# First pair's results held in DRAM by rows and copied out later, one more residual tile, Layer 1 sums by units of one group

## The chip, the core and the metric

The kernel runs on one core of one Trainium2 chip. The metric is device time of one execution in microseconds. TensorE is called PE, VectorE DVE, ScalarE ACT, GpSimd POOL and SyncE SP. SP and ACT each issue DMA transfers into a queue of their own (in the profile, q1 is SP's and q10 is ACT's); both queues run on the same 16 DMA engines.

## The reference

Two layers of the same form: `x = x + scan(groupnorm(x))`, float32 throughout. The scan passes a 48x48 convolution with five taps, along rows and then along columns, each step adding the convolution of the line before to the next line.

```python
def f(carry, inp):                       # one step of a scan
    nxt = inp + _conv1d(carry, w, b)     # 48 channels, 5 taps, padding 2
    return (nxt, nxt)

# x: (32, 48, 64, 128) = batch, channel, row h, column w
xs = jnp.moveaxis(x, 2, 0)
D = scan(down_w, xs)                     # 63 steps over h, downwards
U = scan(down_w, D reversed)             # 63 steps, upwards
R = scan(right_w, columns of U)          # 127 steps over w, to the right
L = scan(left_w, R reversed)             # 127 steps, to the left

def _gn(v, G=16, eps=1e-5): ...          # mean and variance over 3 channels x 64 x 128 of an image
x = x + conv(_gn(x), L0 weights)
x = x + conv(_gn(x), L1 weights)
```

A layer's second half can begin only when the whole image has been summed, since the norm needs its mean and variance. The steps of one scan depend on each other, so the work is a chain of 2 x 4 scans, and it is filled by working on several images at once.

## The kernel before, in words

**Tiling.** The 32 images are four groups of 8. For the row scans a group is worked on alone: 126 steps, each step on a line of 128 columns. For the column scans two groups, a *pair*, go together: 254 steps (127 to the right, 127 to the left). Eight channels-by-position blocks of 48 are packed into 3 x 128 partitions (the table PIECES gives the ten pieces, of 48, 32 or 16 partitions), and a step is 9 fp32 matmuls into 3 PSUM tiles (L641) and 3 DVE instructions that add bias and input (L650). PE and DVE alternate; nothing else is on this chain.

**Phases.** The table PHASES has twelve: eight of rows (group 0 to 3, layer 0 and 1) and four of columns. In what follows they are numbered from 0: phase 2 and phase 6 are the column scans of layer 0, phase 10 that of layer 1 for the *first pair* (images 0 to 15), phase 11 that of layer 1 for the *second pair*. Phase 11 is the last. PE instructions are named by phase: `step_10r` and `step_10l` are the right and the left scan of phase 10 (layer 1, pair 0), `step_11r` and `step_11l` those of phase 11 (layer 1, pair 1); `step_00r` and `step_01r` open phases 2 and 6; `step_00d` and `step_01d` are the downward scans of phases 0 and 1.

**Storage.** One SBUF tile, `arena`, holds three *slots* (each a half image by rows, or one *quarter* of the columns of a pair) and four staging tiles of 2048 floats per partition. A column phase needs four quarters (j = 0 to 3, 32 columns each) and has three slots: quarter 0 and quarter 3 share a slot, so quarter 0 is written to DRAM (`spill`) once the right scan has passed it and is brought back for the left scan. A quarter is six *units* of 128 partitions x 2048 floats (1.05 MB); unit (o, half) is third o of the partitions for one group of the pair. Row results go to the DRAM tensors `upa` and `upb` (layer 0 and 1), the input in the kernel's order to `xin`, layer 0's result to `mid`. Since a column quarter of `upa` can be read only when every row has been written, the start of a column phase that directly follows the rows of its second group (phases 2 and 6) loads that group in parts (L790 on): first the rows 16 to 63, then 8 to 15, then 0 to 7.

**Results of layer 1** (phases 10 and 11). When the left scan is through with a quarter (order 3, 2, 1, 0), each of its six units gets its residual loaded from `mid` into a staging tile (`load_residual`, on ACT's queue), POOL adds scan result and residual and at the same time puts the elements into the order of the output (`add_permuted`, L614, eight instructions of 128x256), and the sum goes from a second staging tile to the output (`store_result`). Two staging tiles hold residuals, two hold sums. In this version a unit of layer 1 is half of the rows of *both* groups of the pair, so a store is cut into 4 x 3 or 4 x 4 transfers, half of them on SP's queue and half on ACT's. The output has 32 floats (128 bytes) in one piece for one image, channel, row and quarter: 49,152 pieces a quarter, 196,608 a pair. For the last quarter of phase 11 the residuals go into a slot that has come free (`last_loads`), DVE adds, and ACT, POOL and DVE reorder (`last_results`, L872 and L880).

**Order.** Nothing is scheduled at run time. `at(t, fn, ...)` (L720) puts a call on a list with a time t, counted in scan steps from the program's start; before each step is recorded, all calls that are due are recorded (`catch_up`, L1047). This fixes the order on each engine and each queue. A queue issues in that order: an instruction that must wait for data or for a buffer holds up all behind it in its queue. `starts[k]` is the step at which phase k begins; in a column phase `left` is the step at which the left scan begins and `end` the one after its last.

**The first group.** Group 0's input is read, reordered, written to `xin` in DRAM and brought back by rows in the first phase; `move_rows` brings rows in, `scale_rows` applies the norm on ACT (L525), and `take_in` reads group 1's input.

## Time and profile before

| | before |
|---|---|
| median of 10 runs | 4554.6 us (4549.24 to 4560.19) |
| the profiled execution's own time | 4552.77 us |
| its span (first to last instruction) | 4551.0 us |
| mean granted TensorE clock | 0.963 |
| PE busy | 4161.9 us (91%) |
| DVE, ACT, POOL busy | 2183.6, 1183.2, 907.9 us (48%, 26%, 20%) |
| DMA | 661.55 MB, 2124132 packets, of them 2010816 under 512 B |

How to read it: the profile is of one execution. "Busy" is time in which an engine runs an instruction; a row of waits names the engine, the line, what ended the wait, and the time in total. In a timeline, the figure in brackets is the idle time just before the row. In a table of windows, each engine has its busy time and, in brackets, its instructions in that stretch; then come PEclk, the clock that TensorE was granted (1.00 is full speed), the share of time that the 16 DMA engines were busy (over 1 where packets of two queues overlap), and what they moved in GB/s. The DMA view of a window gives packets and bytes, and the transfers issued with their median time to landing. The releaser that a wait names is inferred: "DVE L650" before a matmul can stand for a transfer that came late.

### The profile page before, as it was taken

The numbers are of one execution on the slowest core, as the hardware profiler recorded it, in microseconds if no ns is written. First come the engines' busy times: TensorE is split into PE (matmuls) and PEld (weight loads), VectorE is DVE, ScalarE is ACT, GpSimd is POOL, SyncE is SP. The second block draws the span as 40 slices with busy tenths as digits, with TensorE's granted clock in tenths as the row PEclk, the third lists the DMA queues.
The fourth block names the chain that finished last, engine by engine and source line by source line (L and its number), as shares of the span: only waits on it lengthen the run. The fifth ranks groups of instructions, "written<-read, shape, count | busy, mean of one in ns | idle before, by whom it ended". The sixth has DMA issues, their size and how long they took to land.

```text
span 4551.0 us, 90798 instructions
## 1 busy us (share of the span) xinstructions
PE 4161.9 (91%) x36632; PEld 4130.6 (91%) x36632; DVE 2183.6 (48%) x6594; ACT 1183.2 (26%) x2334; POOL 907.9 (20%) x943
## 2 busy tenths in 40 slices
PE   4889998999999999979999999999999997869980
PEld 2889998999999999979999999999999997869980
DVE  5454443446655444434456654444444443334441
ACT  1553302426776445000025944330000000000000
POOL 4441001314412020000024300000000155500554
PEclk9999998999999999989999999999999998989995
DMA  8989789847979999389038989384790199970799
GB/s 178 175 164 156 114 147 198 198 101 244 215 162 162 159 156 158 67 152 201 2 92 241 205 143 152 49 142 82 119 215 2 22 198 179 206 175 1 155 167 160
DMA packets 2124132, 661.55 MB, mean 145 GB/s; under 512 B 2010816, under 2 KB 2063808, under 8 KB 2092224
## 3 DMA queue, kind: packets, MB, share of 16 engines
q1 hardware_dynamic: 1901312, 573.92, 66.1%
q10 hardware_dynamic: 222400, 81.83, 9.5%
q8 instruction: 288, 4.72, 0.5%
q14 instruction: 132, 1.08, 0.1%
HBM read 378.70 MB, written 277.11 MB: 144 GB/s over the span
## 4 chain that ended last, share of the span: by engine, by line
PE 79%; DMA 12%; SPq 3%; ACT 2%; POOL 1%; issue 1%; ACTq 1%; DVE 1%; POOLq 0%; DVEq 0%
PE step_00r L641 6%; PE step_01r L641 6%; PE step_10r L641 6%; PE step_00l L641 6%; PE step_01l L641 6%; PE step_10l L641 5%; DMA arena<-mid 4%; PE step_11r L641 3%; DMA out<-arena 3%; SPq L182 3%; PE step_11l L641 3%; PE step_11d L641 3%; PE step_02u L641 3%; PE step_10u L641 3%; PE step_11u L641 3%; PE step_12d L641 3%
## 5 line engine op out<-in xcount | busy, mean ns | idle before, releaser
L525 ACT ACTIVATE arena<-arena,offset,scale 128x256 f32<-128x256 f32 (+2 forms) x840 | 594.6, 802 | 445.3 <-DMA arena<-xin 181.3
L614 POOL TENSOR_TENSOR arena<-arena 128x256 f32<-128x256 f32 x336 | 349.5, 1080 | 976.2 <-DVE arena L650 714.5
L482 POOL COPY arena<-arena 112x256 f32<-112x256 f32 x458 | 270.8, 650 | 758.5 <-DMA arena<-in_x 427.0
L880 ACT COPY arena<-arena 128x256 f32<-128x256 f32 x18 | 10.5, 643 | 1474.8 <-DMA out<-arena 1471.8
L594 POOL TENSOR_TENSOR arena<-arena 128x2048 f32<-128x2048 f32 x48 | 217.7, 4562 | 839.3 <-PE step_01l L641 543.6
L641 PE MATMUL step_11r<-arena,wright 128*128 128x128 f32 x2286 | 265.3, 280 | 89.0 <-DVE arena L650 42.1
L641 PEld LDWEIGHTS step_11r<-arena,wright 128*128 128x128 f32 x2286 | 263.5, 196 | 90.8 <-DVE arena L650 59.0
L416 ACT ACTIVATE junk<-arena 128x256 f32<-128x256 f32 x192 | 129.5, 675 | 703.6 <-DMA arena<-xin 563.6
L641 PE MATMUL step_01r<-arena,wright 128*128 128x128 f32 x2286 | 258.7, 277 | 29.5 <-DMA arena<-upa 29.5
L641 PEld LDWEIGHTS step_01r<-arena,wright 128*128 128x128 f32 x2286 | 258.4, 194 | 29.8 <-issue 29.6
L641 PE MATMUL step_00r<-arena,wright 128*128 128x128 f32 x2286 | 258.9, 277 | 28.7 <-DMA arena<-upa 28.7
L641 PEld LDWEIGHTS step_00r<-arena,wright 128*128 128x128 f32 x2286 | 258.5, 194 | 29.1 <-issue 28.9
L641 PE MATMUL step_00l<-arena,wleft 128*128 128x128 f32 x2286 | 256.3, 275 | 0.0
L641 PE MATMUL step_10r<-arena,wright 128*128 128x128 f32 x2286 | 256.1, 275 | 0.0
L641 PEld LDWEIGHTS step_10r<-arena,wright 128*128 128x128 f32 x2286 | 255.7, 192 | 0.3
L641 PEld LDWEIGHTS step_00l<-arena,wleft 128*128 128x128 f32 x2286 | 255.7, 192 | 0.0
L641 PE MATMUL step_01l<-arena,wleft 128*128 128x128 f32 x2286 | 255.4, 275 | 0.0
L641 PE MATMUL step_10l<-arena,wleft 128*128 128x128 f32 x2286 | 255.4, 275 | 0.0
L641 PE MATMUL step_11l<-arena,wleft 128*128 128x128 f32 x2286 | 255.4, 275 | 0.0
L641 PEld LDWEIGHTS step_01l<-arena,wleft 128*128 128x128 f32 x2286 | 255.3, 192 | 0.0
L641 PEld LDWEIGHTS step_10l<-arena,wleft 128*128 128x128 f32 x2286 | 255.3, 192 | 0.0
L641 PEld LDWEIGHTS step_11l<-arena,wleft 128*128 128x128 f32 x2286 | 255.3, 192 | 0.0
(173 smaller groups left out, 6990.3 us busy)
## 6 DMA issues: line engine op xcount, KB each, us to landing
xin<-arena SPq DMA_DIRECT2D x96, 384.0 KB, 5.4
arena<-xin SPq DMA_DIRECT2D x96, 384.0 KB, 8.6
mid<-arena SPq DMA_DIRECT2D x96, 384.0 KB, 7.9
arena<-mid SPq DMA_DIRECT2D x192, 192.0 KB, 4.3
upb<-arena SPq DMA_DIRECT2D x192, 192.0 KB, 3.9
arena<-mid ACTq DMA_DIRECT2D x192, 192.0 KB, 4.6
arena<-upb SPq DMA_DIRECT2D x96, 384.0 KB, 10.9
arena<-xin SPq DMA_DIRECT2D x186, 192.0 KB, 4.3
```

The lines of the kernel that those rows point to most:

```text
L182: (queue or nc.sync).dma_start(dst, src)
L416: nc.scalar.activation(junk[:, 0:n], view[:, b], AF.Identity, accum_out=self.sum[:, i, j : j + 1])
L482: copy(dst[:, r, q], src[:, r0 + r, q])
L525: nc.scalar.activation(args[0], args[0], AF.Identity, bias=args[2], scale=args[1])
L594: nc.gpsimd.tensor_tensor(unit, unit, nat, ALU.add)
L614: engines[(2 * a + s) % len(engines)].tensor_tensor(dst[:, a, s], res[:, a, s], inp[:, a, s], ALU.add)
L641: nc.tensor.matmul(part(whole(ps[o]), -s), weights[:, i, FULL * (o - NG * s - i + 1) : FULL * (o - NG * s - i + 2)], part(src(i), s), star ...
L880: copy(dst[:, a, s], src[:, a, s])
```

## The change

Six edits, all in the plan and in the helpers of layer 1's results; no matmul and no DVE instruction of a scan changes.

1. **Units.** In layer 1 a unit is now (third, group), as in layer 0: `load_residual` moves 8 KB rows in 3 or 4 transfers, and `store_result` writes a unit with 3 or 4 transfers, all on SP's queue. The bytes and the 128-byte pieces in the output stay.
2. **Held results.** For the first pair, quarters 2, 1 and 0 are not stored to the output. `hold_result` writes each summed unit as it lies, 128 partitions x 8 KB, to a DRAM tensor (ACT's queue). Later `let_result` copies from DRAM to the output: 48 transfers of 384 KB on SP's queue, listed from 63 steps after phase 11's start on, 1.9 steps apart.
3. **Third residual tile.** The weights of the row scans, which have done their work by then, lie in one tile `downs`; 2048 of its 2304 floats per partition serve as third tile for residuals in both column phases of layer 1.
4. **A gate on ACT.** Ten steps into the left scan of phases 10 and 11, ACT copies one element that the left scan writes at its seventh step; ACT's residual loads stand behind it.
5. **Phases 2 and 6.** The second group's rows 32 to 63 are loaded 31 steps before the phase, rows 16 to 31 13 steps before it; they went together 13 steps before.
6. **First group.** Rows 56 to 63 are brought in together with 48 to 55, ahead of group 1's first input, and scaled in two halves, due 26 and 32 steps into phase 0 (one call due at 34 before).

Three places show the order. In the rows, `out<-held` is a copy from DRAM to DRAM, `mid` the residuals, `upb` and `upa` row results, `spill` quarter 0.

SP's queue at the end of phase 11's loads, before the left scan. Before, the stores of the second pair follow the loads directly:

```order
L182 DMA arena<-upb_97 32x2048
L182 DMA arena<-upb_97 48x2048 x2
L182 DMA arena<-upb_98 32x2048
L182 DMA arena<-upb_98 48x2048 x2
L182 DMA out<-arena 48x16x32 x2
L182 DMA out<-arena 32x16x32
```

Now:

```order
L192 DMA arena<-upb_96 32x2048
L192 DMA arena<-upb_96 48x2048 x2
L192 DMA arena<-upb_97 32x2048
L192 DMA arena<-upb_97 48x2048 x2
L192 DMA out<-held_108 384x8x32 x8
L192 DMA out<-held_109 384x8x32 x8
L192 DMA out<-held_110 384x8x32 x8
L192 DMA out<-held_111 384x8x32 x8
L192 DMA out<-held_112 384x8x32 x8
L192 DMA out<-held_113 384x8x32 x8
L192 DMA out<-arena 384x8x32 x2
```

The 48 copies stand between the last load of phase 11 and the first store of its results, which is behind them in the queue.

ACT's queue in phase 10's left scan. Before, the rows of two units: residual loads and a store's half in turn:

```order
L182 DMA arena<-mid_87 16x1024
L182 DMA arena<-mid_88 16x1024
L182 DMA out<-arena 48x16x32 x2
L182 DMA out<-arena 32x16x32
L182 DMA out<-arena 48x16x32 x2
L182 DMA out<-arena 32x16x32
L182 DMA arena<-mid_87 16x1024
L182 DMA arena<-mid_88 16x1024
L182 DMA arena<-mid_87 48x1024
L182 DMA arena<-mid_88 48x1024
```

Now, in quarter 2:

```order
L192 DMA held_108<-arena 128x2048
L192 DMA arena<-mid_86 32x2048
L192 DMA arena<-mid_86 48x2048 x2
L192 DMA held_109<-arena 128x2048
L192 DMA downs<-mid_87 32x2048
L192 DMA downs<-mid_87 48x2048 x2
```

A unit's store has become one transfer to DRAM, with a residual load of larger rows between two of them; every third residual goes to `downs`.

ACT's queue ahead of phase 2. Before:

```order
L525 ACTIVATE arena<-arena,offset_2822,scale_2821 128x256 x96
L182 DMA arena<-upa_92 48x1536 x2
L182 DMA arena<-upa_92 32x1536
L182 DMA arena<-upa_92 16x1536
L182 DMA arena<-upa_92 48x1536 x2
L182 DMA arena<-upa_92 16x1536
```

Now:

```order
L535 ACTIVATE arena<-arena,offset_2851,scale_2850 128x256 x96
L192 DMA arena<-upa_91 48x1024 x2
L192 DMA arena<-upa_91 32x1024
L192 DMA arena<-upa_91 16x1024
L192 DMA arena<-upa_91 48x1024 x2
L192 DMA arena<-upa_91 16x1024
```

Two thirds of each early load now stand 18 steps earlier; ten transfers of 512 floats follow them at the old place.

The diff:

```diff
--- before.py
+++ after.py
@@ -136,7 +136,9 @@
     arena = const([FULL, 3 * SLOT + 4 * UNIT], "arena")
     slot = [arena[:, i * SLOT : (i + 1) * SLOT] for i in range(3)]
     stage = arena[:, 3 * SLOT :].rearrange("p (i n) -> p i n", i=4)
-    wt = {k: const([FULL, NG, NG * FULL], f"w{k}") for k in ("down0", "down1", "right", "left")}
+    wt = {k: const([FULL, NG, NG * FULL], f"w{k}") for k in ("right", "left")}
+    downs = const([FULL, 2, NG, NG * FULL], "downs")
+    wt |= {f"down{i}": downs[:, i] for i in range(2)}
     bd = const([FULL, NG, 2, 3], "bd")
     mask_sb = const([P, P], "mask_sb")
     maskp = const([P, NG, FULL], "maskp")
@@ -161,6 +163,14 @@
         dram.tile([2 * NG, FULL, UNIT], F32, tag=f"spill{i}", name=f"spill{i}")
         for i in range(4)
     ]
+    HELD = (2, 1, 0)
+    held = {
+        (j, half): dram.tile([NG, FULL, UNIT], F32, tag=f"held{j}{half}", name=f"held{j}{half}")
+        for j in HELD
+        for half in range(2)
+    }
 
     def by_row(t, e, h0, h1):
 
@@ -565,28 +575,12 @@
         else:
             dma(there, here)
 
-    HH = NH // 2
     def load_residual(k, j, i, nat):
         _, layer, pair = PHASES[k]
-        if layer == 0:
-            o, half = UNITS[i]
-            t = source[0][2 * pair + half]
-            for e, c0, c1, p0 in pieces(o):
-                dma(nat[p0 : p0 + c1 - c0], by_col(t, e, j)[c0:c1])
-            return
-        o, r = divmod(i, 2)
-        view = nat.rearrange("p (s n) -> p s n", s=2)
-        part = slice(r * HH * LINE, (r + 1) * HH * LINE)
+        o, half = UNITS[i]
+        t = source[layer][2 * pair + half]
         for e, c0, c1, p0 in pieces(o):
-            for s in range(2):
-                dma(
-                    view[p0 : p0 + c1 - c0, s],
-                    by_col(source[1][2 * pair + s], e, j)[c0:c1, part],
-                    nc.scalar,
-                )
+            dma(nat[p0 : p0 + c1 - c0], by_col(t, e, j)[c0:c1], nc.scalar if layer else None)
 
     def add_residual(k, j, i, nat):
         o, half = UNITS[i]
@@ -602,29 +596,41 @@
                 quarter(k, j)[p0 : p0 + c1 - c0, half, o],
             )
 
-    def add_permuted(k, j, i, nat, perm, engines):
-        o, r = divmod(i, 2)
-        res = quarter(k, j)[:, :, o].rearrange(
-            "p s (a e k b) -> p a s b k e", a=NH, e=E8, b=GB
-        )[:, r * HH : (r + 1) * HH]
-        inp = nat.rearrange("p (s a e k b) -> p a s b k e", s=2, a=HH, e=E8, b=GB)
-        dst = perm.rearrange("p (a s b k e) -> p a s b k e", a=HH, s=2, b=GB, e=E8)
-        for a in range(HH):
-            for s in range(2):
-                engines[(2 * a + s) % len(engines)].tensor_tensor(
-                    dst[:, a, s], res[:, a, s], inp[:, a, s], ALU.add
-                )
+    def by_image(t):
+        return t.rearrange("p (a e k b) -> p a b k e", a=NH, e=E8, b=GB)
+    def by_w(t):
+        return t.rearrange("p (a b k e) -> p a b k e", a=NH, b=GB, e=E8)
+    def add_permuted(k, j, i, nat, perm):
+        o, half = UNITS[i]
+        res = by_image(quarter(k, j)[:, half, o])
+        for a in range(NH):
+            nc.gpsimd.tensor_tensor(by_w(perm)[:, a], res[:, a], by_image(nat)[:, a], ALU.add)
+    def in_output(j, g, e):
+        t = out[g * GB : (g + 1) * GB].rearrange("b c (a e) w -> e (c a) b w", e=E8)
+        return t[e, :, :, j * WQ : (j + 1) * WQ]
 
     def store_result(k, j, i, perm):
         pair = PHASES[k][2]
-        o, r = divmod(i, 2)
-        both = out[2 * pair * GB : 2 * (pair + 1) * GB]
-        dst = both.rearrange("b c (a e) w -> e a c b w", e=E8)[..., j * WQ : (j + 1) * WQ]
-        src = perm.rearrange("p (a b n) -> p a b n", a=HH, b=2 * GB)
-        for a in range(HH):
-            for e, c0, c1, p0 in pieces(o):
-                to = nc.sync if a < HH // 2 else nc.scalar
-                dma(dst[e, r * HH + a, c0:c1], src[p0 : p0 + c1 - c0, a], to)
+        o, half = UNITS[i]
+        for e, c0, c1, p0 in pieces(o):
+            dst = in_output(j, 2 * pair + half, e)[c0 * NH : c1 * NH]
+            src = perm[p0 : p0 + c1 - c0].rearrange("p (a b n) -> p a b n", a=NH, b=GB)
+            dma(dst.rearrange("(c a) b n -> c a b n", a=NH), src)
+    def hold_result(j, i, perm):
+        o, half = UNITS[i]
+        dma(held[j, half][o], perm, nc.scalar)
+    def let_result(j, half, e):
+        src = held[j, half].rearrange("o p (a b n) -> (o p a) b n", a=NH, b=GB)
+        dma(in_output(j, half, e), src[e * C * NH : (e + 1) * C * NH])
 
 
     def step(key, weights, b_at, src, inp, dst, whole, part):
@@ -794,7 +800,8 @@
         for i in range(n):
             if follows(k) and UNITS[i][1] == 1:
                 other = nc.scalar
-                at(t0 - 13 + i, load_unit, k, 0, i, 2, NH, 0, E8, other)
+                at(t0 - 31 + i, load_unit, k, 0, i, 4, NH, 0, E8, other)
+                at(t0 - 13 + i, load_unit, k, 0, i, 2, 4, 0, E8, other)
                 at(t0 - 6 + i / n, load_unit, k, 0, i, 1, 2, 0, E8, other)
                 at(t0 - 1.5, load_unit, k, 0, i, 0, 1, E8 // 4, E8, other)
                 at(t0, load_unit, k, 0, i, 0, 1, 0, E8 // 4, other)
@@ -822,6 +829,8 @@
             stats = ResultStatsV(f"r{2 * pair}"), ResultStatsA(f"r{2 * pair + 1}")
         tiles = [stage[:, i] for i in range(4)]
         nats, perms = (tiles, None) if layer == 0 else (tiles[0:2], tiles[2:4])
+        if layer:
+            nats.append(downs.rearrange("p i g n -> p (i g n)")[:, 0:UNIT])
         ahead = len(nats)
 
         for u, (t, j, i) in enumerate(units):
@@ -842,13 +851,23 @@
                     at(t + 1, stats[1].take, j, o, unit)
             elif not (final and j == 0):
                 perm = perms[u % 2]
-                at(t, add_permuted, k, j, i, nat, perm, [nc.gpsimd])
-                at(t + 5, store_result, k, j, i, perm)
+                at(t, add_permuted, k, j, i, nat, perm)
+                if final or j not in HELD:
+                    at(t + 5, store_result, k, j, i, perm)
+                else:
+                    at(t + 5, hold_result, j, i, perm)
         if layer == 0:
             t = units[-1][0] + 14
             g = 2 * pair
             spread(t, scaling(f"r{g}", 1, g, stats[0], r_masks), 1)
             spread(t + 20, scaling(f"r{g + 1}", 1, g + 1, stats[1], r_masks), 1)
+        if layer:
+            at(left + 10, nc.scalar.copy, junk[:, 0:1], quarter(k, 3)[:, 0, 0, RUN - 1 : RUN])
+        if layer and not final:
+            todo = [(j, half, e) for j in HELD for half in range(2) for e in range(E8)]
+            for n, what in enumerate(todo):
+                at(end + 63 + 1.9 * n, let_result, *what)
         if final:
             at(left + 97, last_loads, k)
             at(end + 4, last_results, k)
@@ -865,19 +884,14 @@
     def last_results(k):
 
         for i, nat in enumerate(last_tiles(k)):
-            o, r = divmod(i, 2)
-            part = slice(r * HH * LINE, (r + 1) * HH * LINE)
-            unit = quarter(k, 0)[:, :, o, part]
-            nat = nat.rearrange("p (s n) -> p s n", s=2)
+            o, half = UNITS[i]
+            unit = quarter(k, 0)[:, half, o]
             nc.vector.tensor_tensor(unit, unit, nat, ALU.add)
-            src = unit.rearrange("p s (a e k b) -> p a s b k e", a=HH, e=E8, b=GB)
             perm = stage[:, i % 4]
-            dst = perm.rearrange("p (a s b k e) -> p a s b k e", a=HH, s=2, b=GB, e=E8)
-            for a in range(HH):
-                for s in range(2):
-                    eng = (nc.scalar, nc.gpsimd, nc.vector)[(2 * a + s) % 8 % 3]
-                    copy = eng.copy if eng is nc.scalar else eng.tensor_copy
-                    copy(dst[:, a, s], src[:, a, s])
+            for a in range(NH):
+                eng = (nc.scalar, nc.gpsimd, nc.vector)[a % 3]
+                copy = eng.copy if eng is nc.scalar else eng.tensor_copy
+                copy(by_w(perm)[:, a], by_image(unit)[:, a])
             store_result(k, 0, i, perm)
 
 
@@ -1032,14 +1046,14 @@
         scale_rows(0, 24, 32)
         move_rows(0, 32, 48, False)
         scale_rows(0, 32, 40)
-        move_rows(0, 48, 56, False)
+        move_rows(0, 48, 64, False)
         take_in(1, 0, nats1[0])
 
     in_order(first_group)
     at(starts[0] + 10, scale_rows, 0, 40, 48)
-    at(starts[0] + 20, move_rows, 0, 56, 64, False)
     at(starts[0] + 22, take_in, 1, 16, nats1[1])
-    at(starts[0] + 34, scale_rows, 0, 48, 64)
+    at(starts[0] + 26, scale_rows, 0, 48, 56)
+    at(starts[0] + 32, scale_rows, 0, 56, 64)
 
     agenda.sort(key=lambda a: a[:2])
     done = 0
```

## The prediction

> **What bounds the kernel now.** I read the table of windows first, one window for each scan of the last two phases and one for the tail (columns: window, length, busy time of PE, PEld, DVE, ACT, POOL, then granted clock, DMA share, GB/s).
>
> ```profile
> 3560.00:3815.00 255.00, 255.00 (x2286) 255.00 (x2285) 121.85 (x381) 0.00 (x0) 113.64 (x109) 1.00 0.72 139
> 3815.00:4170.00 355.00, 266.01 (x2296) 264.21 (x2295) 123.24 (x383) 0.00 (x0) 86.33 (x84) 0.87 0.76 150
> 4170.00:4425.00 255.00, 254.84 (x2283) 254.65 (x2281) 121.78 (x381) 0.00 (x0) 116.59 (x112) 1.00 0.69 136
> 4425.00:4551.00 126.00, 0.00 (x0) 0.00 (x0) 23.35 (x19) 10.46 (x18) 49.44 (x50) 0.51 1.02 162
> ```
>
> A column scan that nothing disturbs is PE's: 255 us for 127 steps, 2.01 a step. The right scan of phase 11 takes 355, 100 too many, and after the last step 126 us pass with no matmul while the DMA share is 1.02. These are the two places with much to win. Then the PE timeline over the 355 us, with the idle time and its releaser in brackets:
>
> ```profile
> 3789.78 25.62 PE L641 MATMUL step_10l<-arena,wleft 128*128 128x128 f32 x228
> 3829.47 1.22 PE L641 MATMUL step_11r<-arena,wright 128*128 128x128 f32 x4 [13.62 <-DMA out<-arena]
> 3848.34 66.57 PE L641 MATMUL step_11r<-arena,wright 128*128 128x112 f32 x570 [17.65 <-DMA arena<-mid]
> 3918.90 1.65 PE L641 MATMUL step_11r<-arena,wright 128*128 128x128 f32 x6 [3.98 <-DVE arena L650]
> 3936.20 65.16 PE L641 MATMUL step_11r<-arena,wright 128*128 128x112 f32 x568 [15.65 <-DMA arena<-mid]
> 4009.98 0.79 PE L641 MATMUL step_11r<-arena,wright 128*128 128x128 f32 x2 [8.62 <-DVE arena L650]
> 4031.06 1.65 PE L641 MATMUL step_11r<-arena,wright 128*128 128x128 f32 x6 [20.29 <-DVE arena L650]
> 4041.88 127.69 PE L641 MATMUL step_11r<-arena,wright 128*128 128x112 f32 x1126 [9.18 <-DVE arena L650]
> ```
>
> Three waits, before steps 1, 32 and 64 (32 steps are 576 matmuls): each is for the next quarter of phase 11, which is loaded into a slot that phase 10's results must leave first. They are 31.3, 19.6 and 38.1 us, 89.0 together. By the page's groups the scan's matmuls are also 10 us longer in sum than those of the left scan, which has no waits and the full clock; so the waits cost 99.
>
> ```profile
> L641 PE MATMUL step_11r<-arena,wright 128*128 128x128 f32 x2286 | 265.3, 280 | 89.0 <-DVE arena L650 42.1 <-DMA arena<-mid 33.3 <-DMA out<-arena 13.6
> L641 PE MATMUL step_11l<-arena,wleft 128*128 128x128 f32 x2286 | 255.4, 275 | 0.0
> ```
>
> The DMA view of the stretch says what the loads wait behind:
>
> ```profile
> DMA  3998889999897999999999999999999999999999
> DMA packets 216494, 88.35 MB, mean 198 GB/s; under 512 B 205738, under 2 KB 205738, under 8 KB 211882
> ```
>
> From 3620 to 4066 the DMA engines are busy throughout, and 205,738 of the packets are small: phase 10's output, which by the code is 196,608 pieces of 128 bytes. Between that and the next stretch the engines are idle (4080 to 4215):
>
> ```profile
> DMA  0000000000000000000000000000000000000000
> DMA packets 12, 0.18 MB, mean 1 GB/s; under 512 B 0, under 2 KB 0, under 8 KB 0
> ```
>
> **Edit 2, 3 and 4 in the right scan of phase 11.** Prices first, each from a window with one kind of transfer: the last stores (4500 to 4540), residual loads alone (4421 to 4449), loads of 128-byte pieces from DRAM (1520 to 1540), and spills of 128 partitions x 8 KB to DRAM (3362 to 3378).
>
> ```profile
> DMA packets 52002, 6.51 MB, mean 163 GB/s; under 512 B 52000, under 2 KB 52000, under 8 KB 52000
> ```
>
> ```profile
> DMA packets 1840, 5.28 MB, mean 189 GB/s; under 512 B 551, under 2 KB 551, under 8 KB 1840
> ```
>
> ```profile
> DMA packets 24988, 3.17 MB, mean 159 GB/s; under 512 B 24987, under 2 KB 24987, under 8 KB 24987
> ```
>
> ```profile
> DMA packets 649, 4.74 MB, mean 296 GB/s; under 512 B 72, under 2 KB 72, under 8 KB 72
> ```
>
> Three quarters are 147,456 pieces; at 52,002 in 40 us they take 113 us of the DMA engines. They leave the stretch. In come 18 held units of 1.05 MB, 18.9 MB; the form is that of a spill, 64 us at 296 GB/s. That window includes some loads and an idle start, so 64 is the upper bound; I take 55. The gate keeps two units' residuals of phase 11 (2.1 MB, 11 us at 189 GB/s) out of the stretch; ACT issued them there (its timeline, 12 transfers):
>
> ```profile
> 3995.39 14.33 ACTq L182 DMA_DIRECT2D arena<-mid  x12
> ```
>
> Net: 113 - 55 + 11 = 69 us less DMA work ahead of the third wait. It ended at 4041.9; 69 earlier is 3973. Without waits step 64 is due at 3815 + 64 x 2.01 = 3944, so by work alone 29 us of waiting stay, and the gain is 69.
>
> It should be more, since the DMA engines can also do this work faster. In the last left scan, where the same mechanism runs, POOL shows how a unit is paced:
>
> ```profile
> 4383.28 8.31 POOL L614 TENSOR_TENSOR arena<-arena 128x256 f32<-128x256 f32 x8 [5.31 <-DMA arena<-mid]
> 4396.86 8.30 POOL L614 TENSOR_TENSOR arena<-arena 128x256 f32<-128x256 f32 x8 [5.26 <-DMA arena<-mid]
> 4410.01 8.31 POOL L614 TENSOR_TENSOR arena<-arena 128x256 f32<-128x256 f32 x8 [4.86 <-DMA arena<-mid]
> 4458.09 8.15 POOL L614 TENSOR_TENSOR arena<-arena 128x256 f32<-128x256 f32 x8 [39.76 <-DMA out<-arena]
> ```
>
> A unit takes 13.2 us, 8.3 of adding and 5 of waiting for a residual, since a tile is loaded only when its last user is done. With three tiles the next residual is there. A held unit needs 5.5 us of loading (1.05 MB at 189) and about 3 of holding: 8.6, no more than POOL's 8.3. A quarter then takes 6 x 8.6 = 52 us, and the scan gives one every 32 steps, 64 us. So results keep up with the scan from quarter 2 on, and the lag that is left at quarter 0 is what quarter 3 (still stored directly) and the spill leave behind. I take 12 us of waiting and of slow clock instead of 99: **-87**, with -55 (the work alone, and a slower pace of the residuals) and -99 (no waiting) as bounds. What is late next is PE itself.
>
> **The copies to the output** cost the sum nothing, by this cover, which SP's timeline bounds:
>
> ```profile
> 4016.23 42.86 SPq L182 DMA_DIRECT2D arena<-upb  x30
> 4233.94 22.44 SPq L182 DMA_DIRECT2D out<-arena  x20
> ```
>
> The last load was issued at 4059, 17 us after the third wait, and with some 8 us to land it is through 25 after it; now that is about 3944 + 12 + 25 = 3981. The first store comes 64 us after the right scan's end at 4170; now that end is near 3815 + 255 + 12 = 4082, and the store at 4146. Between lie 165 us, less 17 for three residual units. No row shows a copy of this size from DRAM to DRAM. Lower bound: it is paced by its writes, 147,456 at the stores' rate, 113 us. Upper bound: each piece pays its read and its write, 113 + 118 (at 24,988 in 20 us) = 231. The two rows say that a piece costs the same whichever end DRAM is on, about 12.5 ns of one of the 16 engines, so the descriptor and not the memory sets it: I take 113, and it fits into 148. If the cover is gone, SP's queue is the place: the second pair's stores stand behind the 48 copies.
>
> **Edit 1 and 3 in the left scan and the tail.** The bytes do not change. The cycle could fall from 13.2 us a unit to what the DMA engines need: 8,192 pieces at 1,300 per us are 6.3, the residual 5.5, together 11.8. Over 17 units that is -24 us; the residual prefetched for a third unit adds -6. Against it: the last quarter is stored through one queue, 1,249 pieces per us instead of 1,300, +1.5. POOL's 39.8 us of waiting at 4458 are no idle time of the DMA engines, they load the residuals of quarter 0 (those 5.28 MB at 189 GB/s); stores of three units can now run beside it. In this stretch the share is already high, so I take **-10**, bounds -30 and +1.5.
>
> **Edit 5.** Phases 2 and 6 open with a wait each:
>
> ```profile
> PE step_01r L641 <- DMA arena<-upa: 29.5, 1, 29.5
> PE step_00r L641 <- DMA arena<-upa: 28.7, 1, 28.7
> ```
>
> For the first of them, ACT's timeline and two windows:
>
> ```profile
> 655.36 39.31 ACTq L182 DMA_DIRECT2D arena<-upa  x30
> ```
>
> ```profile
> 640.00:650.00 10.00, 10.00 (x92) 10.00 (x91) 4.89 (x15) 0.00 (x0) 0.00 (x0) 1.00 0.65 104
> 660.00:670.00 10.00, 10.00 (x92) 10.00 (x91) 4.80 (x15) 0.00 (x0) 0.00 (x0) 1.00 1.20 198
> ```
>
> The early loads, 2.36 MB in the first ten of ACT's thirty transfers, start at 655, when the rows' last stores want the same engines (share 1.20). Two thirds, 1.57 MB or 8 us at 189 GB/s, now go ahead of that, where the share leaves room. The final stores and loads of rows 0 to 7 stay, so not more than 8 us of each wait can go. I take 6 each: **-12**, bounds -16 and 0. ACT has nothing behind these loads before phase 2.
>
> **Edit 6.** The wait for rows 48 to 63 (20.4 of the 36.8 us below) goes: both loads now precede group 1's input. But the input pipeline of group 1 (SP, POOL and DMA, none waiting for PE) sets when phase 1 can scan its rows, and PE already waits for it there:
>
> ```profile
> PE step_00d L641 <- DVE arena L650: 36.8, 3, 20.4
> PE step_01d L641 <- DVE arena L650: 6.6, 2, 6.3
> ```
>
> 20 us won in phase 0 become 20 us more of waiting in phase 1; only what the earlier start of the input gives is kept. **-2**, bounds -20 and +5 (group 1's first input is issued after ten more loads).
>
> **Sum:** -87 - 10 - 12 - 2 = -111. The profiled execution took 4552.8 (its span 4551.0 and 1.8 around it), so the like of it 4441.8; the median of the runs is 1.8 above it, so the forecast is **4443.6**.
>
> **Rivals.** *The waits stay in part (0.14).* The results are paced by the residual loads, which reach 189 GB/s and no more, and the third quarter's load still comes late. For it: work alone leaves 29 us; against it: three tiles. -55 instead of -87: 4475.6. *More goes (0.12).* No waiting and a tail that reaches the 11.8 us cycle: -99 - 30 - 12 - 2 = -143, 4411.6. *The copies pay twice (0.09).* 231 us against 148 of cover, 83 late on SP's queue, and the tail, which the DMA engines set, ends 83 later: 4526.6. For it is that both ends are DRAM; against it the equal price of the two single-ended rows. [...] *Slower (0.05).* The same place and mechanism at a higher price: a read that DRAM answers late holds its write, and a piece takes three times its 12.3 ns, 339 us in all, 191 late: 4634.6. It decides from 148 + 111 = 259 us on, 28 ns a piece. For it nothing in the profile speaks but that no such copy is shown. *The change does less than it says:* the queue order above shows that it moves the stores, so this is only the first rival's case.
>
> **How the numbers follow.** Forecast 0.60, rivals 0.14, 0.12, 0.09, 0.05. The forecast's own range is 4425 to 4465. For 8 in 10 I reach from a little below the better case's 4411.6 to beyond the first rival: 4405 to 4500; outside are the copies' rivals and the best of the gains. About 0.2% (9 us) can be told from no change. Faster: all but the last rival and a remainder, 0.93; within 0.2%: 0.02; slower: 0.05.
>
> **What would show it.** Right: `step_11r` idle near 12 instead of 89; POOL's units in phase 10 some 8.6 us apart in quarters 2 to 0; a block of `out<-held` with the DMA share near 1 inside the right scan of phase 11, 113 us long, done before the first store; POOL's 5 us gaps smaller in the last left scan; the waits of `step_00r` and `step_01r` near 23; `step_00d` 20 less and `step_01d` more by nearly as much. Wrong: copies that still run when the first store is due, a third wait over 30 us, or a tail longer than 126.

## The result, and the profile after

The kernel before took 4554.1 us (median of 29 runs), the changed one 4457.65 us (8 runs, 4446.66 to 4464.99). The ratio is 0.9787, with a 95% interval of 0.9779 to 0.9796: 96 us less. The forecast was 4443.6, 111 us less, with a range of 4405 to 4500. The profiled execution took 4454.03 us, its span 4452.2.

Where the time went shows in the first matmul of each scan on PE's timelines of the two kernels:

| from ... to | before, us | after, us | difference |
|---|---|---|---|
| start to `step_00r` | 704.1 | 699.6 | -4.5 |
| `step_00r` to `step_01r` | 1321.2 | 1314.4 | -6.9 |
| `step_01r` to `step_11r` | 1789.9 | 1789.4 | -0.5 |
| right scan of phase 11 | 354.2 | 268.4 | -85.8 |
| left scan of phase 11 and tail | 381.6 | 380.5 | -1.1 |
| span | 4551.0 | 4452.2 | -98.8 |

The table of windows of the changed kernel, one row for each scan of the last two phases and one for the tail (window, length, busy time of PE, PEld, DVE, ACT, POOL, then granted clock, DMA share, GB/s):

```profile
3548.10:3803.40 255.30, 255.30 (x2289) 255.30 (x2288) 122.11 (x381) 0.19 (x1) 116.61 (x113) 1.00 0.78 176
3803.40:4071.80 268.40, 257.55 (x2289) 257.06 (x2288) 122.42 (x381) 0.00 (x0) 83.10 (x80) 0.98 1.02 220
4071.80:4327.20 255.40, 255.38 (x2288) 255.19 (x2286) 122.01 (x381) 0.19 (x1) 107.97 (x104) 1.00 0.84 159
4327.20:4452.20 125.00, 0.00 (x0) 0.00 (x0) 27.44 (x19) 10.78 (x18) 59.65 (x58) 0.51 0.92 161
```

The right scan of phase 11 takes 268 us instead of 355, and its clock is 0.98 instead of 0.87. The tail is as long as before, but its DMA share fell from 1.02 to 0.92: the DMA engines are no longer busy all through it. PE's timeline of the changed kernel shows what is left of the three waits (a step's 9 matmuls are 18 rows in the profile, so 32 steps are 576):

```profile
3803.38 65.38 PE L647 MATMUL step_11r<-arena,wright 128*128 128x128 f32 x584
3869.41 64.61 PE L647 MATMUL step_11r<-arena,wright 128*128 128x112 f32 x576 [0.66 <-DVE arena L656]
3944.22 127.69 PE L647 MATMUL step_11r<-arena,wright 128*128 128x112 f32 x1126 [10.19 <-DVE arena L656]
```

The first wait (31.3 us before) is gone, the second is 0.7 instead of 19.6, the third 10.2 instead of 38.1. PE's other waits in the changed kernel (engine, line, releaser: us in total, times, longest):

```profile
PE step_00r L647 <- DMA arena<-upa: 27.0, 1, 27.0
PE step_01r L647 <- DMA arena<-upa: 23.4, 1, 23.4
PE step_00d L647 <- DVE arena L656: 19.7, 3, 9.8
...
PE step_11r L647 <- DVE arena L656: 10.9, 2, 10.2
PE step_00u L647 <- DVE arena L656: 8.5, 1, 8.5
...
PE step_01d L647 <- DVE arena L656: 5.3, 1, 5.3
...
PE step_01d L647 <- issue: 5.0, 1, 5.0
```

The waits of `step_00r` and `step_01r` fell by 1.7 and 6.1 us. The 20 us wait in `step_00d` is gone. In its place `step_00u` waits 8.5 us (0.2 before), and `step_01d` 10.3 in all (8.2 before).

Next the stretch in which the DMA engines are busy throughout, in the kernel before and, below it, in the changed one (windows, columns as above):

```profile
3620.00:4066.00 446.00, 357.01 (x3112) 355.29 (x3112) 166.32 (x518) 0.00 (x0) 199.97 (x192) 0.89 1.01 198
```

```profile
3620.00:3965.00 345.00, 334.15 (x2976) 333.76 (x2975) 159.30 (x497) 0.00 (x0) 189.84 (x183) 0.99 1.00 242
```

It is 101 us shorter; counted from the start of phase 11 (3815.2 and 3803.4) it ends after 251 and 162 us, 89 earlier. The share is 1.0 in both, but 242 GB/s are moved instead of 198, and the small pieces are a quarter of the 205,738 of before (the DMA view of the changed kernel's stretch):

```profile
DMA packets 61632, 83.38 MB, mean 242 GB/s; under 512 B 52246, under 2 KB 52246, under 8 KB 52246
```

After it, SP's timeline:

```profile
3934.41 29.63 SPq L192 DMA_DIRECT2D arena<-upb  x23
3965.80 132.92 SPq L192 DMA_DIRECT2D out<-held  x48
4142.19 27.81 SPq L192 DMA_DIRECT2D out<-arena  x7
```

The copies are all issued by 4098.7, 43 us before the first store. In a window that holds only copies (3980 to 4080) the DMA view says

```profile
DMA packets 123097, 15.81 MB, mean 158 GB/s; under 512 B 123088, under 2 KB 123088, under 8 KB 123088
...
q1 hardware_dynamic: 123088, 15.68, 105.0%
```

(the second row is SP's queue, with its share of the 16 engines; it is over 1 with one queue alone, so packets of one queue overlap in the record too). That is 1231 pieces a us, 120 us for the 147,456 pieces.

### The profile page after: what moved, and what is told of

Same layout as the page of the kernel before. It is cut to its first block, busy times and chain, and to the rows that moved or that the text cites. A ratio compares the mean times of both kernels' runs of the same rounds, so it can differ in the third digit from the quotient of the medians.

```text
span 4452.2 us, 89843 instructions
## 1 busy us (share of the span) xinstructions
PE 4156.6 (93%) x36632; PEld 4126.9 (93%) x36632; DVE 2187.1 (49%) x6594; ACT 1190.3 (27%) x2360; POOL 909.5 (20%) x943
## 3 DMA queue, kind: packets, MB, share of 16 engines
q14 instruction: 125, 1.02, 0.1%
## 5 line engine op out<-in xcount | busy, mean ns | idle before, releaser
L610 POOL TENSOR_TENSOR arena<-arena 128x256 f32<-128x256 f32 x224 | 235.1, 1093 | 782.4 <-DVE arena L656 661.0
L647 PE MATMUL step_11r<-arena,wright 128*128 128x128 f32 x2286 | 257.7, 276 | 10.9 <-DVE arena L656 10.9
L647 PEld LDWEIGHTS step_11r<-arena,wright 128*128 128x128 f32 x2286 | 257.1, 193 | 11.3 <-DVE arena L656 11.2
```

The lines of the kernel that those rows point to most:

```text
L610: nc.gpsimd.tensor_tensor(by_w(perm)[:, a], res[:, a], by_image(nat)[:, a], ALU.add)
L647: nc.tensor.matmul(part(whole(ps[o]), -s), weights[:, i, FULL * (o - NG * s - i + 1) : FULL * (o - NG * s - i + 2)], part(src(i), s), star ...
```

## Experiments

Each edit is made to the changed kernel unless something else is said. Times are medians; "ratio" is to the kernel before, measured beside each of them, and the changed kernel's own ratio of 0.9787 (0.9779 to 0.9796) is what it is to be held against.

**Nothing held (edit 2 undone).**

```diff
-    HELD = (2, 1, 0)
+    HELD = ()
```

> The changed kernel with nothing held: quarters 2, 1 and 0 of the first pair go straight to the output again; units of one group, third tile, gate and edits 5 and 6 stay. Theory of the prediction (the 113 us of 128-byte pieces in front of the loads make the waits): the waits of step_11r come back, 70 to 89 us of idle time instead of 10.9, and the time is 4525 to 4545. Rival (larger rows and the third tile speed the results): step_11r idle at most 40, time at most 4490.

4558.6 us, ratio 1.0013 (1.0002 to 1.0024). PE's waits:

```profile
PE step_11r L647 <- DVE arena L656: 68.1, 6, 17.0
PE step_11r L647 <- DMA arena<-upb: 41.8, 3, 20.8
```

The waits are back, 109.9 us of them, more than the 89.0 of the kernel before and more than the theory said. So the whole gain of the change hangs on edit 2: without it the other five edits together stand 0.13% above the kernel before. The bytes of the three quarters are the same either way; what edit 2 changes is that they leave in rows of 8 KB and not in pieces of 128 bytes while the loads wait. Something among the other five makes the right scan worse, which the next run looks for.

**Edit 1 alone on the kernel before.** Units of one group, stores on SP only; all other edits undone.

```diff
-            nats.append(downs.rearrange("p i g n -> p (i g n)")[:, 0:UNIT])
-            at(left + 10, nc.scalar.copy, junk[:, 0:1], ...)
-    HELD = (2, 1, 0)
+    HELD = ()
+    (edits 5 and 6 as before)
```

> The kernel before with edit 1 alone: units of one group, stores of 3 or 4 transfers on SP's queue only; no held results, two residual tiles, no gate, loads of phases 2 and 6 and of the first group as before. Without the held results the changed kernel stood at 4558.6 with 109.9 us of waits in step_11r, 21 more than before. Theory (the stores, now all on SP's queue, stand ahead of phase 11's loads there): these 21 us come with edit 1, step_11r idle 100 to 115, time 4560 to 4575. Rival (third tile or gate bring them): step_11r idle 85 to 95, time 4545 to 4558.

4598.2 us (two runs), ratio 1.0098 (1.0078 to 1.0118), 45 us above the kernel before and beyond what either theory gave. PE's waits, and the DMA share from the first result to the last load of phase 11:

```profile
PE step_11r L647 <- DMA arena<-upb: 60.2, 4, 18.9
PE step_11r L647 <- DVE arena L656: 58.3, 5, 19.4
```

```profile
3620.00:4094.00 474.00, 355.51 (x3076) 353.23 (x3075) 164.81 (x513) 0.00 (x0) 198.98 (x192) 0.86 0.95 184
```

118.5 us of waits instead of 89.0, and a tail of 136 us instead of 126. The bytes are those of before; the share falls from 1.01 to 0.95, over a stretch 28 us longer, so the engines do the same work with idle time in it. So edit 1 brings the worse right scan. That it is the single queue, in which phase 11's loads stand behind the stores, fits the releaser `arena<-upb`, which the kernel before did not have; that is argued and not shown, since row form and queue were not separated.

**Two residual tiles (edit 3 undone).**

```diff
-            nats.append(downs.rearrange("p i g n -> p (i g n)")[:, 0:UNIT])
```

> The changed kernel with two residual tiles instead of three. Theory of the prediction (the results are paced by the residual, 5 us of waiting a unit, which the third tile takes away): 18 units get slower by up to 5 us each, step_11r idle 35 to 45 instead of 10.9, time near 4485. Rival (in the changed kernel held units stand 14.4 us apart with a DMA share of 1.0, so the DMA engines' work sets the pace and not the tile): step_11r idle 10 to 18, time within 8 us of 4457.7.

4473.6 us, ratio 0.9837 (0.9816 to 0.9859): 16 us slower, between the two expectations. The right scan keeps its gain:

```profile
PE step_11r L647 <- DVE arena L656: 14.2, 2, 10.1
```

Of the profiled difference (spans 4468.5 and 4452.2), 9 us lie in the tail, 134.1 us instead of 125.0, and 5 in the right scan. So the third tile is not what lets the held results keep up; it is worth most at the end.

**No copies.** Of the 48 copies only the first is made; 47 of the 48 blocks of the first pair's quarters 2, 1 and 0 are left out of the output.

```diff
             for n, what in enumerate(todo):
-                at(end + 63 + 1.9 * n, let_result, *what)
+                if n % 48 == 0:
+                    at(end + 63 + 1.9 * n, let_result, *what)
```

> The changed kernel with one of the 48 copies instead of all: 47 of the 48 blocks of the first pair's quarters 2, 1 and 0 are left out of the output, nothing else. Theory of the prediction (the copies lie wholly under work of others): within 4 us of 4457.7. Rival (they hold up the last loads or the first stores, or the DMA engines' idle time would have been used by the last left scan): 8 us or more below it.

4459.0 us, ratio 0.9801 (0.9783 to 0.9819). The copies cost nothing that can be measured: 120 us of DMA time lie wholly under the scan.

**Copies twice.**

```diff
                 at(end + 63 + 1.9 * n, let_result, *what)
+                at(end + 63 + 1.9 * n + 0.95, let_result, *what)
```

> The changed kernel with each of the 48 copies from DRAM to the output issued twice: 294,912 pieces instead of 147,456. One set took about 121 us (1215 pieces a us) and left some 33 us of idle DMA time before the first store. Theory (the copies are free only as long as the cover lasts; past it every microsecond is paid behind SP's queue): 88 us too many, up to 28 of which the idle time of the DMA engines in the last left scan can take back: +60 to +88, so 4518 to 4546, and the right scan of phase 11 as before. Rival (the stores catch up in the last left scan, which has slack): less than +30, below 4488.

4615.3 us (two runs), ratio 1.0138 (1.0118 to 1.0159): 158 us slower, about twice what the theory gave. SP's timeline, one row of PE's, and the DMA view of 4000 to 4100 (digits are the busy share of 2.5 us slices in tenths):

```profile
3962.52 351.18 SPq L192 DMA_DIRECT2D out<-held  x96
4313.80 63.54 SPq L192 DMA_DIRECT2D out<-arena  x20
4377.51 21.06 SPq L192 DMA_DIRECT2D arena<-spill  x4
```

```profile
4393.63 0.79 PE L647 MATMUL step_11l<-arena,wleft 128*128 128x128 f32 x2 [131.44 <-DVE arena L656]
```

```profile
DMA  9169399089099099297296693692990990990992
```

The run was not a clean doubling. The second copy of a block writes where the first has written, so SP waits for the first to land before it issues the second (48 waits on `out<-held`, 218.0 us in all between 3950 and 4420). The DMA engines fall idle at each such pair, and 96 copies take 351 us and not 240. What it does show is who pays when the cover is gone. Not only the stores stand behind the copies on SP's queue: quarter 0, which the left scan needs back (`arena<-spill`), is issued at 4377, and PE itself stands for 131 us. The prediction had named the stores alone.

**Second pair's stores on two queues.**

```diff
-            dma(dst.rearrange("(c a) b n -> c a b n", a=NH), src)
+            to = nc.scalar if pair and j < 2 and n % 2 else nc.sync
+            dma(dst.rearrange("(c a) b n -> c a b n", a=NH), src, to)
```

> The changed kernel with every second transfer of the second pair's last two quarters stored through ACT's queue instead of SP's. In the changed kernel the last 74 us of stores run at a DMA share near 0.75, 972 pieces a us between 4423 and 4450, with dips between the transfers of the one queue. Theory 1 (one queue does not keep the engines busy; the tail's term was mis-sized for that): share near 1 and 1250 or more pieces a us in the tail, 8 to 18 us less, 4440 to 4450. Theory 2 (the sum of the DMA work or the chain of adding and reordering bounds the tail): within 3 us of 4457.7.

4456.8 us, ratio 0.9791 (0.9775 to 0.9807): no difference. Yet the last stores do run faster. The same 36 us, near the end, in the changed kernel and in this one:

```profile
4404.00:4440.00 36.00, 0.00 (x0) 0.00 (x0) 9.04 (x8) 5.21 (x9) 9.25 (x11) 0.50 0.81 133
```

```profile
4404.00:4440.00 36.00, 0.00 (x0) 0.00 (x0) 10.34 (x9) 9.62 (x17) 14.37 (x17) 0.50 1.39 172
```

The share over 1 is overlap; what counts is 172 GB/s against 133. Over the whole stretch from 4380 to the end it is 137 against 129. POOL's last addition ends 47.4 us before the end instead of 54.8, so 7.4 us are won there. They were lost before it: POOL's timeline in this kernel has a wait of 25 us where the changed kernel has 4.6 at the same unit.

```profile
4361.55 8.09 POOL L610 TENSOR_TENSOR arena<-arena,downs 128x256 f32<-128x256 f32 x8 [25.08 <-DMA out<-arena]
```

POOL waits there for a tile of sums that a store must leave first. ACT's timeline shows why that store is late:

```profile
4309.62 38.72 ACTq L192 DMA_DIRECT2D arena<-mid  x20
4348.37 0.79 ACTq L192 DMA_DIRECT2D out<-arena  x1
```

The sum in question was done at 4308.7. SP issued its share of the store from 4309.9 on, but ACT's share stands in its queue behind twenty residual loads of the last quarter and goes out at 4348.4. (The expectation of the last run below has it the other way round, loads behind stores.) So both theories hold a part: one queue does leave DMA time unused at the end, and more DMA speed there does not shorten the tail when the second queue makes an earlier store late.

**Loads of phases 2 and 6 as before (edit 5 undone).**

```diff
-                at(t0 - 31 + i, load_unit, k, 0, i, 4, NH, 0, E8, other)
-                at(t0 - 13 + i, load_unit, k, 0, i, 2, 4, 0, E8, other)
+                at(t0 - 13 + i, load_unit, k, 0, i, 2, NH, 0, E8, other)
```

> The changed kernel with the second group's rows 16 to 63 of phases 2 and 6 loaded together 13 steps before the phase, as before the change (edit 5 undone). Theory (the early loads shorten the opening waits of phases 2 and 6; the starts of the scans in the two traces give 2.3 and 6.5 us): step_00r and step_01r wait near 29 each instead of 27.0 and 23.4, and the time is 6 to 12 us above 4457.7. Rival (the last rows bound these waits whatever is loaded early, and the 9 us are differences between two executions): within 3 us of 4457.7.

4469.0 us, ratio 0.9818 (0.9802 to 0.9833), 11 us slower; the interval does not touch that of the changed kernel. Its waits:

```profile
PE step_00r L647 <- DMA arena<-upa: 30.0, 1, 30.0
PE step_01r L647 <- DMA arena<-upa: 29.3, 1, 29.3
```

They are 3.0 and 5.9 us longer than with the edit. The theory holds.

**First group as before (edit 6 undone).**

```diff
-        move_rows(0, 48, 64, False)
+        move_rows(0, 48, 56, False)
...
+    at(starts[0] + 20, move_rows, 0, 56, 64, False)
-    at(starts[0] + 26, scale_rows, 0, 48, 56)
-    at(starts[0] + 32, scale_rows, 0, 56, 64)
+    at(starts[0] + 34, scale_rows, 0, 48, 64)
```

> The changed kernel with rows 56 to 63 of group 0 brought in after the first step of phase 0 and scaled together with 48 to 55, as before the change (edit 6 undone). Theory of the prediction (the input of group 1 sets when phase 1 can go on; a wait won in phase 0 is lost again by phase 1): step_00d gets its 20 us wait back, the waits after it shrink by nearly as much, and the time rises by 0 to 6 us. Rival (the wait in phase 0 is on the path): 12 to 20 us more.

4456.4 us, ratio 0.9790 (0.9776 to 0.9805): no difference. The wait of 20 us is back in phase 0, and the 8.5 us of `step_00u` are gone. This run's row first, then one of DVE's timeline in the changed kernel, where `step_00u` goes on at 312.3:

```profile
PE step_00d L647 <- DVE arena L656: 33.6, 3, 19.6
```

```profile
310.70 1.29 DVE L339 BATCH_NORM_STATS2 bn_x<-arena 112x6 f32<-112x512 f32 x2 [8.49 <-DMA arena<-in_x]
```

`step_00u` starts 17 us later than in the changed kernel (279.6 and 262.9), `step_01d` 6 us later (409.1 and 402.9), `step_01u` 5 us later (550.6 and 545.8). So most of the time won is lost again, and to group 1's input, as the prediction had it, but not where it had it. In the changed kernel DVE, which takes group 1's statistics (`bn_x`) in between, stands 8.5 us for that input and PE with it, in the upward scan of phase 0; of 17 us, 10 are gone before phase 1 begins.

**Without ACT's gates (edit 4 undone).**

```diff
-            at(left + 10, nc.scalar.copy, junk[:, 0:1], quarter(k, 3)[:, 0, 0, RUN - 1 : RUN])
```

> The changed kernel without ACT's gate, so that residuals of phase 11 are loaded as soon as their tiles are free, during the last loads of quarter 0 (edit 4 undone). Theory of the prediction (11 us of DMA work return to the stretch ahead of the third wait; with three tiles 17): the wait of step_11r before step 64 is 18 to 27 instead of 10.2, the time 8 to 17 us higher. Rival (these transfers end up behind the loads anyway, or the earlier residual gives in the last left scan what it takes here): within 4 us.

4500.8 us, ratio 0.9888 (0.9872 to 0.9905): 43 us slower, far beyond both expectations, and not at the place they named. The waits of `step_11r` stay at 11.7 us. PE stands at the opening of phase 10, where the changed kernel has no wait at all:

```profile
3300.66 1.17 PE L647 MATMUL step_10r<-arena,wright 128*128 128x128 f32 x8
3313.02 65.77 PE L647 MATMUL step_10r<-arena,wright 128*128 128x112 f32 x570 [11.19 <-DMA arena<-upb]
3386.92 1.65 PE L647 MATMUL step_10r<-arena,wright 128*128 128x128 f32 x6 [8.13 <-DVE arena L656]
3407.44 12.74 PE L647 MATMUL step_10r<-arena,wright 128*128 128x112 f32 x90 [18.87 <-DVE arena L656]
```

For 190 us before it the DMA engines did almost nothing (a window, then ACT's timeline, then SP's):

```profile
3111.00:3300.00 189.00, 189.00 (x1695) 189.00 (x1695) 90.37 (x282) 0.00 (x0) 0.51 (x1) 1.00 0.03 5
```

```profile
3300.62 1.73 ACTq L192 DMA_DIRECT2D downs<-mid  x4
```

```profile
3303.52 0.77 SPq L192 DMA_DIRECT2D arena<-upb  x2
```

Without the gate nothing holds ACT back, and it comes to phase 10's residual loads more than 200 steps early. Those of the third unit go into `downs`, whose weights PE reads until the row scans end at about 3300.7, so ACT waits there. SP stops at 3110 and goes on 1.2 us after ACT's four transfers have been issued. SP's own row of waits for 3080 to 3330 names those loads, although nothing that SP moves there touches `downs`:

```profile
SPq L192 <- DMA downs<-mid: 195.6, 3, 192.7
```

(In the changed kernel SP waits in this place too, but for DVE and only until 3179.)

The program's rows with the semaphores that each waits for name the link. ACT:

```
456 L192 DMA downs<-mid_86 16x2048 [waits DMAHW5_49,PE_49]
457 L192 DMA downs<-mid_86 48x2048 [waits DMAHW7_49]
```

SP:

```
2116 L192 DMA arena<-upb_95 32x2048 [waits DMAHW4_49]
2117 L192 DMA arena<-upb_95 48x2048 [waits DMAHW5_49]
```

Transfers of both queues report their landing on the same eight semaphores in turn (`DMAHW0` to `DMAHW7`), and a transfer first waits for the one before it on its semaphore. SP's next load has the semaphore of ACT's blocked load.

**Gate kept in phase 10 alone.**

```diff
-            at(left + 10, nc.scalar.copy, junk[:, 0:1], ...)
+            final or at(left + 10, nc.scalar.copy, junk[:, 0:1], ...)
```

> The changed kernel with ACT's gate kept in phase 10 and taken out of phase 11 only. Without both gates the time rose by 43 us, of which 38 were waits at the opening of phase 10: SP issued nothing from 3110 to 3303, until ACT's residual load into the third tile, which waits for the row scans' last matmul, had gone. Theory (the two queues share the semaphores on which transfers signal that they have landed, and a load that is blocked holds one of them; in phase 11 no such load is blocked): within 4 us of 4457.7, and the wait of step_11r before step 64 stays 8 to 13. Prediction's theory (the gate keeps 11 us of residual loads out of the stretch): 8 to 11 us slower.

4460.5 us, ratio 0.9792 (0.9778 to 0.9807), 2.9 us above the changed kernel and within its spread, and the waits of `step_11r` are 9.9 us. In phase 11 the gate does nothing that can be measured; in phase 10 it is worth about 40 us. That the stop came from the load into `downs` is shown by SP's row of waits and by the order in time; that the shared semaphore is the link is read from the program's waits, and no run gave the two queues semaphores of their own.

**Quarter 3 held too.**

```diff
-    HELD = (2, 1, 0)
+    HELD = (3, 2, 1, 0)
...
-                at(end + 63 + 1.9 * n, let_result, *what)
+                at(end + 63 + 1.42 * n, let_result, *what)
```

> The changed kernel with quarter 3 of the first pair held too: 64 copies instead of 48, listed 1.42 steps apart. Theory (the waits that are left come from quarter 3's 49,152 pieces, 38 us of DMA work, which become a spill of 6.3 MB, 16 to 21): the third wait of step_11r, 10.2 us, goes; the copies take 196,608 / 1215 = 162 us and still end before the first store near 4125; time 4444 to 4450. Rival 1 (the last wait has another cause): within 3 us of 4457.7. Rival 2 (cover gone): slower by 5 us or more, the first store of the second pair late.

4451.4 us, ratio 0.9770 (0.9754 to 0.9786). The right scan of phase 11 has no wait left and the full clock:

```profile
3812.40:4068.00 255.60, 255.60 (x2289) 255.53 (x2289) 122.38 (x381) 0.00 (x0) 74.59 (x72) 1.00 1.02 219
```

The last wait did come from quarter 3's pieces: 13 us are won there. At the end some are given back: in the profiled execution the tail is 130.1 us, against 118.9 to 125.0 in seven others that have the same work there. The copies now run until the first stores are due. By the medians 6 us remain, and the two intervals overlap, so that this version is faster than the changed kernel is likely and not certain.

**Quarter 3 held, and the last quarter's stores on two queues.** The edit of the two queues, for `j == 0` alone.

> The kernel with quarter 3 held too, and with every second transfer of the last quarter's stores alone (quarter 0 of the second pair) on ACT's queue, where no residual load stands behind them any more. In the changed kernel the DMA share between 4380 and 4452 is 0.79; with two queues on the last two quarters 1,300 pieces a us were reached from 4404 on, but residual loads were held up behind ACT's stores. Theory (one queue leaves 20 us of DMA time unused at the end, and nothing else stands in the way): 5 to 10 us below the 4451.4 of the kernel with quarter 3 held, 4441 to 4446. Rival (adding and reordering, or the wait of ACT's reordering behind its stores, set the end): within 3 us of 4451.4.

4454.1 us, ratio 0.9792 (0.9779 to 0.9806): nothing gained that shows. In the profiled execution, the fastest of the five, the time after POOL's last addition is 49.8 us instead of 55.4. With five runs between 4440.9 and 4456.5, a few microseconds more or less cannot be told here.

## Why the prediction was right, and where its steps failed

The sign and the place were right, the time 14 us (0.3%) too low. Against the profiled execution (forecast 4441.8, measured 4454.0) the 12 us part as follows: right scan 1.2, left scan and tail 8.9, everything ahead 2.1.

**Right scan, -87: measured -85.8, but not by its working.** Waits and slower matmuls together are 13 us (10.9 and 2.3) where 12 were taken. The step "69 by work alone" was too small: the stretch of full DMA share ends 89 us earlier. The large rows probably went faster than before, which the step did not allow for. An estimate from the two DMA views: with the small pieces at 1300 a us, the rest of the stretch moved 76.7 MB in 305 us, some 250 GB/s, and before, by the same working, 62.0 MB in 288 us, some 215. What makes them faster (longer rows, the kind of transfer, the queue) no run separates. The step that was to supply the rest failed: "a held unit needs 8.6 us, with three tiles the next residual is there". POOL's timeline of the changed kernel, first and last of the last sixteen of the eighteen held units:

```profile
3708.78 8.29 POOL L610 TENSOR_TENSOR arena<-arena,downs 128x256 f32<-128x256 f32 x8 [6.71 <-DMA held<-arena]
...
3924.58 8.37 POOL L610 TENSOR_TENSOR arena<-arena,downs 128x256 f32<-128x256 f32 x8
```

Fifteen distances in 215.8 us are 14.4 us each. The DMA share is 1.00 all the while, and with two tiles the scan waits hardly more (14.2): that fits units paced by all that the engines carry, the loads of phase 11 among it, and not by the tile. An underestimate of the DMA work saved and a wrong reason for a faster pace came to nearly the right sum; that the two met so closely is luck.

**Edit 4, 11 us in that term: measured nothing in phase 11**, and about 40 us where the prediction did not look. It had costed the gate only as DMA work moved out of a stretch. It did not ask what the new third tile makes ACT wait for in phase 10, and who stands behind a blocked load.

**The copies, 0: right.** 120 us instead of 113, and no time won without them. The rival by which each piece pays its read and its write (231 us) falls. Sixteen engines at 1231 pieces a us are 13.0 ns of one engine for a copied piece, and 12.3 for a stored one at 1300. The Trainium skill, DMA: Bandwidth & Descriptors, section "Why small descriptors are slow (HBM only)", names two reasons for the penalty of small pieces, a fixed overhead per packet and 32 bytes of descriptor metadata per DMA operation. Both are counted by packet or operation and not by the ends that lie in DRAM, and the 13.0 and 12.3 ns agree with that; no run here moves small pieces within SBUF alone. The cover was worked out with loads that land after 8 us; in the window 4055 to 4080 of the kernel before they took 10.4 to 11.2, which changes nothing.

**Left scan and tail, -10: measured -1.1** in the two profiled executions. The tail with this work varied from 118.9 to 125.0 us in seven profiles, against 126.2 in that of before, so -1 to -7 is what can be said. POOL's last addition divides the tail (before, then the changed kernel):

```profile
4496.21 8.15 POOL L614 TENSOR_TENSOR arena<-arena 128x256 f32<-128x256 f32 x8 [4.29 <-DMA out<-arena]
```

```profile
4388.91 8.47 POOL L610 TENSOR_TENSOR arena<-arena,downs 128x256 f32<-128x256 f32 x8 [1.89 <-DMA out<-arena]
```

It ends 79.5 us after the left scan before and 70.2 after the change, so 9.3 us are won. From there to the end it takes 46.6 us before and 54.8 after, so 8.2 are lost. The failed step is the price of one queue, taken as +1.5 from a rate of 1,249 pieces a us: in all eleven profiles with the last stores on SP's queue alone this last part takes 53.9 to 55.6 us, and in the three with two queues 46.6 to 49.8. The stores from 4380 to the end ran at a DMA share of 0.79. The 9.3 us are the third tile's: with two tiles POOL's last addition ends 79.7 us after the scan again. That tile, taken as -6, is worth 16 us in all by the medians; edit 1, from which the prediction took a gain as well, costs 45 us alone, 10 of them in the tail.

**Phases 2 and 6, -12: measured -11** by undoing the edit, -8 by the waits alone (1.7 and 6.1, where 6 each were taken). **First group, -2: nothing measurable.** `step_00d` waits 17.1 us less, near the 20 forecast, but `step_01d` only 2.1 more: the step that failed is the place, since `step_00u` in phase 0 takes 8.3 of it.

Of the rivals none came. "The waits stay in part" rested on the 69 us of DMA work saved; the stretch became 89 shorter.

## What to carry to other kernels

Small pieces in front of loads that the critical engine waits for can be moved out of the way by writing them to DRAM in large rows and copying later, if a stretch with idle DMA engines follows: here 120 us of copies cost nothing and the scan that waited became 86 us shorter. Before a queue is given all of one kind of transfer, look at what stands behind it: the same bytes, in units of one group and all on one queue, cost 45 us until the detour took them away. And a load that is issued early into a buffer that is still in use blocks more than its own queue where transfers of several queues share the semaphores on which they report.

## What the runs showed that was not expected

- A blocked load on ACT's queue stopped SP's queue for 190 us (3111 to 3300, DMA share 0.03) with no dependence in the data between them. The Trainium skill, DMA: Bandwidth & Descriptors, section "Why a DMA increments its semaphore by 16 and not by 1", advises a semaphore for each slot in flight, so that a count is not filled by a later transfer; this program keeps counts apart by making each transfer wait for the one before it on its semaphore, and the 190 us are what that can cost; no run here tests the page's own reason.
- Copies of 128-byte pieces from DRAM to DRAM ran at 1231 pieces a us, within 6% of the stores from SBUF (1300).
- Loads, held results, spills and one quarter's stores together reached 242 GB/s over 345 us; residual loads alone had 189.
- Stores of up to 3072 pieces on one queue moved 133 GB/s near the end (4404 to 4440); with every second transfer on the other queue the same 36 us moved 172. After POOL's last addition one queue took 54 to 56 us, two queues 47 to 50.
